# Four-tile layer blocks from one operand buffer in a recommender kernel: one comparison a step, one feature buffer, later reductions

## The chip, the cores and the metric

The kernel runs on one core of a Trainium2 chip. The metric is device time in microseconds (us), the median over several runs. Engines: PE (TensorE matmul), PEld (its weight loads), DVE (VectorE), ACT (ScalarE), POOL (GpSimd, which issues the gathers) and SP (SyncE, which issues the plain DMAs).

## What is computed

For each of 16384 rows: the mean of 32 rows of a 50000 x 300 table, the means of 20 rows of three tables of width 64, four single rows of width 64, all side by side (748 features), three relu layers and a sigmoid, with a "wide" sum of scalars added before the sigmoid.

```python
tok = word_emb[token_idx].mean(axis=1)
e1 = emb_mh1[mh1_idx].mean(axis=1)      # 1000 rows; mh2 5000, mh3 10000
...
o1 = emb_oh1[oh1_idx]                   # 100 rows; oh2 50, oh3 20, oh4 1000
...
emb = jnp.concatenate([tok, e1, e2, e3, o1, o2, o3, o4], axis=1)
wide = (wide_mh1[mh1_idx].sum(axis=(1, 2)) + ... + wide_oh4[oh4_idx][:, 0])[:, None]
h = jax.nn.relu(emb @ W1 + b1)          # 748 -> 1024
h = jax.nn.relu(h @ W2 + b2)            # 1024 -> 512
h = jax.nn.relu(h @ W3 + b3)            # 512 -> 256
return jax.nn.sigmoid(h @ Wd + bd + wide)
```

## The kernel before

A tile is 128 rows; there are 128 tiles. The kernel is one long schedule written out by hand (`manual_schedule`): a loop of 1424 steps, 11 to a tile and 16 more at the end (`WAKE`), in which the order of the calls is the order of the instructions on each engine. Every engine works off its own queue in order. Five streams run side by side, shifted against each other:

- **Token gather** (`tokens`, L249; `add_up`, L237). POOL issues 4096 indirect DMAs of 128 table rows (L259), two to a buffer `tok_rows`, with six buffers. Three groups of two later, DVE adds them up in `own` (L241, L243, L247); the last addition of a tile writes `g_tok`. The gathers are spread evenly over the steps.
- **Counts** (`one_hots`, L318; `counts`, L336). The small tables are not gathered. For each row, DVE compares its 64 keys with an iota (L326, twice a step: 6 rows of the low key, `row`, and 6 of the slice number, `slice`), ACT scales half of the `row` part (L333), PE multiplies the two (L344, 6 products a step), and ACT packs the counts into `cnt` (L347). `row` and `slice` have two buffers each; the comparison for step i+1 is issued in step i.
- **Sums from counts** (`small_sums`, L353). One tile later, PE multiplies the counts with the small tables kept on chip, 138 products a tile (L363), in four groups of fields, in the order of `SMALL`; each group collects in `pg`, which has one buffer, and DVE reduces it into the feature buffer `g` (L369). `sums_by_step` spreads them over the steps, one group's end to a step at most.
- **Transposes** (`Block.add_small`, L401; `Block.add_tokens`, L415). Four and three PE transposes per tile (L405, L408, L424, L425), evicted by DVE in three and two instructions (L409, L412, L413; L426, L427) into `x_small` and `x_tok`, which have two buffers each.
- **Layers** (`mlp`, L475; `layer`, L453). When the tiles of a block of three (`LAYER_TILES`) are in place, its 48 + 32 + 8 products and the two of the output run with 384 columns (L462, L487), ACT evicts each (L471), paced over the steps until the next block is due (`ready`, L547; `begin`, `left`). 42 blocks of three and two of one tile. If a block is not through when the next is ready, the rest is issued at once (`layers.finish`). The last tile's first three chunks are multiplied early (`early_part`, L435).

At the start, PE splits the small tables into three bf16 terms (`convert_tables`, L171), paced by `TABLE_PACE`. Index loads (`load_indices`, L270) are made once for four tiles on SP; `lookup_keys` and `key_columns` prepare their keys.

The functions, with the line numbers of the profile:

Of the kernel before, what the change touches and what calls it, by code (L numbers as in the profile page):

```python
# [8 lines left out]
F32 = mybir.dt.float32  # L9
# [16 lines left out]
TOK_BUFS = 6  # L26
WAKE = 16
EARLY = 3
BLOCK = 512
LAYER_TILES = 3  # L30
LAST_TILES = 2
# [8 lines left out]
TABLE_PACE = 1.3  # L40
# [5 lines left out]
SMALL = ("o4", "e1", "e2", "e3", "o1", "o2", "o3")  # L46
WIDE_IN_FRONT = ("mh1", "mh3", "oh2")
G_COLS = 7 * ROW
# [7 lines left out]
def kernel(  # L56
# [27 lines left out]
    tables = {"o4": oh4, "e1": mh1, "e2": mh2, "e3": mh3, "o1": oh1, "o2": oh2, "o3": oh3}  # L84
    slices, n_h = {}, 0
    for f in SMALL:
# [9 lines left out]
    ohp = ctx.enter_context(tc.tile_pool(name="onehot", bufs=2))  # L96
    cp = ctx.enter_context(tc.tile_pool(name="counts", bufs=2))
    gp = ctx.enter_context(tc.tile_pool(name="g", bufs=2))
    wp = ctx.enter_context(tc.tile_pool(name="wide", bufs=2))
    xsp = ctx.enter_context(tc.tile_pool(name="x_small", bufs=2))  # L100
    xtp = ctx.enter_context(tc.tile_pool(name="x_tok", bufs=2))
# [7 lines left out]

    chunk_rows = [  # L110
        [(300, 428)],
        [(428, 556)],
        [(556, 684)],
        [(684, 748), (256, 300)],
        [(0, 128)],
        [(128, 256)],
    ]
    chunk_k = [sum(b - a for a, b in rows) for rows in chunk_rows]
    NK = len(chunk_rows)

# [4 lines left out]
    scale = const.tile([P, 3], F32, name="scale")  # L125
# [3 lines left out]

# [18 lines left out]


# [61 lines left out]

# [9 lines left out]
    def load_weights():  # L221
        for k, rows in enumerate(chunk_rows):
            at = 0
            for a, b in rows:
                nc.sync.dma_start(out=w1_sb[at : at + b - a, k, :], in_=w1[a:b, :])
                at += b - a
        nc.sync.dma_start(out=w2_sb, in_=w2.rearrange("(k p) m -> p k m", p=P))
        nc.sync.dma_start(out=w3_sb, in_=w3.rearrange("(k p) m -> p k m", p=P))
        for sb, dram in ((wd_sb, wd), (b1_sb, b1), (b2_sb, b2), (b3_sb, b3), (bd_sb, bd)):
            nc.sync.dma_start(out=sb, in_=dram)  # L230

    n_groups = N_TOK // TOK_GROUP
    n_all = B // P * n_groups + TOK_LAG
    sums_of = {}
    token_indices = {}

    def add_up(t, q, rows):  # L237
# [4 lines left out]
        else:  # L242
            nc.vector.tensor_add(tok_sum, tok_sum, a)  # L243
            to = tok_sum
            if q == n_groups - 1:
                to = sums_of[t] = gp.tile([P, TOK_D], F32, name="g_tok")
# [23 lines left out]
    def load_indices(blk):  # L270
# [7 lines left out]
        ix = keyp.tile([P, NSUB // 2, 2, N_SMALL], I32, name="ix")  # L278
        for s in range(NSUB):
            nc.sync.dma_start(  # L280
                out=ix[(s % 2) * HALF : (s % 2 + 1) * HALF, s // 2],
# [7 lines left out]
    def lookup_keys(ix):  # L289

        pairs = NSUB // 2
        low = keyp.tile([P, pairs, 2, N_SMALL], I32, name="low", tag="low")
        nc.vector.tensor_single_scalar(low, ix, P - 1, op=ALU.bitwise_and)
        nc.vector.tensor_single_scalar(ix, ix, 7, op=ALU.logical_shift_right)
        keys = keyp.tile([P, pairs, 2, 2 * N_SMALL], BF16, name="keys", tag="keys")
        for r in range(pairs):
            view = keys[:, r].rearrange("p w (f c) -> p w f c", f=2)
            nc.vector.tensor_copy(view[:, 0], low[:, r])
            nc.vector.tensor_add(view[:, 1], ix[:, r], first)
        return keys  # L300

    def key_columns(keys):


        pairs = NSUB // 2
        pk = ps_h.tile([P, pairs, 2, P], BF16, name="pk", tag="ph")
        for r in range(pairs):
            for w in range(2):
                nc.tensor.transpose(pk[:, r, w, :], keys[:, r, w, :], ident_bf)
        sc = scp.tile([P, pairs, 2, 2, HALF, 2], BF16, name="sc")  # L310
        n = pairs * 2 * P
        nc.vector.tensor_copy(
            sc.rearrange("p r w t b d -> p (r w t b) d"),
            pk.rearrange("p r w b -> p (r w b)").unsqueeze(2).to_broadcast([P, n, 2]),
        )
        return sc

    def one_hots(sc, s, i):  # L318
# [3 lines left out]
        row1 = ohp.tile([P, ONEHOT, P], BF16, name="row1")  # L322
        slice1 = ohp.tile([P, ONEHOT, n_h], BF16, name="slice1")
        for w, (one, n) in enumerate(((row1, P), (slice1, n_h))):
            shape = [P, rows, n // 2, 2]
            nc.vector.tensor_tensor(  # L326
                one[:, 0:rows, :].rearrange("p i (n d) -> p i n d", d=2),
                iota[:, 0:n].rearrange("p (n d) -> p n d", d=2).unsqueeze(1).to_broadcast(shape),
                sc[:, s // 2, w, s % 2, b : b + rows, :].unsqueeze(2).to_broadcast(shape),
                ALU.is_equal,  # L330
            )
        upper = row1[HALF:P, 0:rows, :]
        nc.scalar.activation(upper, upper, AF.Copy, scale=UPPER)  # L333
        return row1, slice1

    def counts(cnt, hot, i):  # L336
# [5 lines left out]
        for k in range(rows):  # L342
            at = k % n * n_h
            nc.tensor.matmul(  # L344
                pc[:, k // n, at : at + n_h], hot[0][:, k, :], hot[1][:, k, :], start=True, stop=True
            )
# [6 lines left out]
    def small_sums(g, cnt):  # L353
# [3 lines left out]
        for i in (0, 2, 4, 6):  # L357
            pair = SMALL[i : i + 2]
            pg = ps_g.tile([P, 2, 3 * ROW], F32, name="pg")
            for j, f in enumerate(pair):  # L360
                h0, h1 = slices[f]
                for h in range(h0, h1):
# [3 lines left out]
                    yield 1  # L366
            at = i * ROW
            n = len(pair)
            nc.vector.tensor_reduce(  # L369
                g[:, at : at + n * ROW].rearrange("p (f d) -> p f d", f=n),  # L370
                pg[:, 0:n, :].rearrange("p f (c d) -> p f d c", c=3),
                AX.X,
                ALU.add,
            )
            yield None

    def wide_term(g):
# [4 lines left out]
            g[:, EMB : EMB + 6 * ROW].rearrange("p (c d) -> p c d", d=2 * ROW)[:, :, 0:2],  # L382
# [3 lines left out]
        nc.vector.tensor_add(g[:, EMB : EMB + 1], wide, g[:, G_COLS - 1 : G_COLS])  # L386

    class Block:
# [3 lines left out]
        def __init__(self, first, n):  # L392
            self.first, self.n, self.missing = first, n * P, 2 * n
            self.small = xsp.tile([P, 4, N], F32, name="x_small")
            self.wide = wp.tile([1, N], F32, name="wide_row")
            self.tok = None

        def columns(self, t):
            return slice((t - self.first) * P, (t - self.first + 1) * P)

        def add_small(self, t, g):  # L401

            at = self.columns(t)
            pt = ps_h.tile([P, 4, P], F32, name="pt", tag="ph")
            nc.tensor.transpose(pt[:, 3, :], g[:, 0:P], ident)  # L405
            for k in range(3):
                c = (1 + 2 * k) * ROW + 1
                nc.tensor.transpose(pt[:, k, :], g[:, c : c + P], ident)  # L408
            nc.vector.tensor_tensor(  # L409
                self.small[:, 0:3, at], pt[:, 0:3, :], scale.unsqueeze(2).to_broadcast([P, 3, P]), ALU.mult  # L410
            )
            nc.vector.tensor_copy(self.small[0:EMB, 3, at], pt[0:EMB, 3, :])  # L412
            nc.vector.tensor_copy(self.wide[:, at], pt[EMB : EMB + 1, 3, :])  # L413

        def add_tokens(self, t, g):  # L415


            if self.tok is None:
                self.tok = xtp.tile([P, 2, N], F32, name="x_tok")
            at = self.columns(t)  # L420
            rest = TOK_D - 2 * P
            pt = ps_h.tile([P, 3, P], F32, name="pt", tag="ph")
# [242 lines left out]
```

## Time and profile before

| what | value |
|---|---|
| median of 10 runs | 5194.51 us (5191.93 to 5196.4) |
| profiled execution | 5194.04 us, span from first to last instruction 5192.3 us |
| granted PE clock, mean | 0.983 |
| DMA | 652 MB, mean 126 GB/s |
| matmuls of the layers (L462) | 7744 records, two to each fp32 product |

The page lists busy times per engine, the span in 40 slices, the chain of work that ended last, and the costliest groups of instructions with the idle time in front of them and what ended it. Of the chain that ended last, PE has 28% of the span, DMA 25%, DVE 19%, "issue" 16% and POOL 9%. In a group's line the first number after the bar is the busy time in all, the second the mean length of one instruction in ns; overlapping matmuls make that length greater than the distance from one start to the next. Timeline lines read: start, length, engine, line, operation, number of instructions merged, and in brackets the idle time before and what ended it.

### The profile page before, as it was taken

What the parts mean: (1) busy time and instruction counts of PE and PEld (TensorE: products, weight loads), DVE (VectorE), ACT (ScalarE), POOL (GpSimd) and SP (SyncE); (2) the same over time, 40 slices, a digit from 0 to 9 for tenths busy, and PEclk for the clock granted to TensorE, in tenths of its full rate; (3) what the DMA queues carried; (4) which work ended last, traced back from release to release, by engine and by line L of the source; (5) the groups of instructions that cost most, each with busy time, mean ns of one, the idle gap of its engine ahead of it and who ended that gap; (6) DMA issues with size and microseconds to landing.
All of it is one profiled execution on the core that took longest, in us unless ns stands there. A gap on an engine that the chain in (4) does not pass through costs nothing.

```text
span 5192.3 us, 94821 instructions
## 1 busy us (share of the span) xinstructions
PE 4846.5 (93%) x34940; PEld 3557.5 (69%) x34940; DVE 3854.5 (74%) x8481; ACT 2758.4 (53%) x3538; POOL 3877.1 (75%) x4103
## 2 busy tenths in 40 slices
PE   7899999999999999999999999999999999999999
PEld 5676676667666766766776667666667666676667
DVE  7777777777777777777777777777777777777772
ACT  6555555555555555555555555555555555555551
POOL 7777777777777777777777777777777777777774
PEclk9999999999999999999999999999999999999999
DMA  7444444444444444444444444444444444444442
GB/s 198 124 126 126 124 127 126 124 125 126 125 124 125 126 125 125 127 126 124 126 125 126 124 125 126 126 124 127 125 124 126 125 125 124 125 126 126 124 124 67
DMA packets 252899, 652.00 MB, mean 126 GB/s; under 512 B 119035, under 2 KB 119591, under 8 KB 252435
## 3 DMA queue, kind: packets, MB, share of 16 engines
q0 software_dynamic: 196608, 629.41, 45.2%
q1 hardware_dynamic: 55827, 16.53, 1.4%
q8 instruction: 276, 4.52, 0.4%
q14 instruction: 188, 1.54, 0.1%
HBM read 645.59 MB, written 0.07 MB: 124 GB/s over the span
## 4 chain that ended last, share of the span: by engine, by line
PE 28%; DMA 25%; DVE 19%; issue 16%; POOL 9%; ACT 1%; DVEq 0%; SPq 0%; POOLq 0%; ACTq 0%
DMA tok_rows<-in_word_emb_dram,it 24%; PE ph L462 16%; POOL tok_rows L259 9%; PE pg L363 8%; DVE own L247 6%; DVE own L243 4%; DVE slice L326 3%; PE pc L344 2%; DVE row L326 2%; PE po L487 1%; DVE g L369 1%; DVE wide_row L413 0%; DVE own L241 0%; DVE x_small L427 0%; DVE x_small L412 0%
## 5 line engine op out<-in xcount | busy, mean ns | idle before, releaser
L259 POOL DMA_INDIRECT tok_rows<-in_word_emb_dram,it x4096 | 3876.2, 946 | 1277.9 <-issue 760.8
L333 ACT ACTIVATE row<-row 64x768 bf16<-64x768 bf16 (+1 forms) x1408 | 1155.3, 821 | 1570.6 <-DVE row L326 1551.9
L363 PE MATMUL pg<-terms,cnt 128*128 128x195 bf16 x17664 | 1764.1, 249 | 227.0 <-DVE g L369 225.9
L363 PEld LDWEIGHTS <-cnt 128*128 128x128 fp8e3 x17664 | 1529.0, 98 | 181.8 <-issue 175.1
L347 ACT ACTIVATE cnt<-pc 128x828 uint16<-128x828 f32 (+1 forms) x1408 | 1191.8, 846 | 165.3 <-PE pc L344 130.7
L462 PE MATMUL ph<-h,w_sb 128*128 128x384 f32 (+1 forms) x3520 | 1254.0, 495 | 0.5 <-ACT h L471 0.5
L247 DVE TENSOR_TENSOR own<-own,tok_rows 128x300 f32<-128x300 f32 x1792 | 856.9, 478 | 469.6 <-DMA tok_rows<-in_word_emb_dram,it 425.5
L243 DVE TENSOR_TENSOR own<-own,tok_rows 128x300 f32<-128x300 f32 x1920 | 918.0, 478 | 261.2 <-DMA tok_rows<-in_word_emb_dram,it 204.8
L462 PE MATMUL ph<-x_small,w_sb 128*128 128x384 f32 (+1 forms) x2784 | 1012.2, 488 | 6.2 <-DVE x_small L409 3.3
L344 PEld LDWEIGHTS <-row 128*128 128x128 bf16 x8192 | 599.9, 98 | 587.4 <-issue 282.5
L462 PEld LDWEIGHTS ph<-h,w_sb 128*128 128x128 f32 x3520 | 633.5, 197 | 387.0 <-issue 107.1
L326 DVE TENSOR_TENSOR row<-own,sc 128x768 bf16<-128x768 bf16 (+1 forms) x1408 | 761.8, 541 | 128.0 <-PE pc L344 28.5
L326 DVE TENSOR_TENSOR slice<-own,sc 128x828 bf16<-128x828 bf16 (+1 forms) x1408 | 795.9, 565 | 0.0
L344 PE MATMUL pc<-slice,row 128*128 128x138 bf16 x8192 | 740.7, 225 | 53.2 <-ACT row L333 52.5
L471 ACT ACTIVATE h<-ph,b_sb 128x384 f32<-128x384 f32 (+1 forms) x612 | 350.0, 572 | 626.0 <-PE ph L462 601.0
L462 PEld LDWEIGHTS ph<-x_small,w_sb 128*128 128x128 f32 x2784 | 487.3, 192 | 246.4 <-issue 21.1
L462 PE MATMUL ph<-x_tok,w_sb 128*128 128x384 f32 (+1 forms) x1392 | 533.7, 488 | 0.0
L369 DVE TENSOR_REDUCE g<-pg 128x130 f32<-128x390 f32 (+1 forms) x512 | 258.4, 505 | 95.8 <-PE pg L363 93.8
L462 PEld LDWEIGHTS ph<-x_tok,w_sb 128*128 128x128 f32 x1392 | 243.6, 192 | 113.5 <-issue 6.8
L241 DVE TENSOR_TENSOR own<-tok_rows 128x300 f32<-128x300 f32 x128 | 61.2, 478 | 116.9 <-DMA tok_rows<-in_word_emb_dram,it 115.9
L426 DVE TENSOR_SCALAR x_tok<-pt 128x256 f32<-128x256 f32 x128 | 53.6, 419 | 105.5 <-PE pt L425 105.4
L409 DVE TENSOR_TENSOR x_small<-pt,scale 128x384 f32<-128x384 f32 x128 | 70.2, 549 | 39.1 <-PE pt L408 37.6
(56 smaller groups left out, 875.4 us busy)
## 6 DMA issues: line engine op xcount, KB each, us to landing
tok_rows<-in_word_emb_dram,it POOLq DMA_INDIRECT x4096
ix<-in_idx_dram SPq DMA_DIRECT2D x128, 32.0 KB
w_sb<-in_W_dram SPq DMA_DIRECT2D x6, 512.0 KB
raw<-in_mh_dram SPq DMA_DIRECT2D x4, 682.5 KB
it<-in_idx_dram SPq DMA_DIRECT2D x32, 64.0 KB
w_sb<-in_W_dram SPq DMA_DIRECT2D x1, 2048.0 KB
out_dram<-h SPq DMA_DIRECT2D x42, 1.5 KB
raw<-in_mh_dram SPq DMA_DIRECT2D x2, 227.5 KB
```

The lines of the kernel that those rows point to most:

```text
L243: nc.vector.tensor_add(tok_sum, tok_sum, a)
L247: nc.vector.tensor_add(to, tok_sum, b)
L259: nc.gpsimd.indirect_dma_start(out=rows[:, r * TOK_D : (r + 1) * TOK_D], out_offset=None, in_=word, in_offset=bass.IndirectOffsetOnAxis(ap ...
L326: nc.vector.tensor_tensor(one[:, 0:rows, :].rearrange("p i (n d) -> p i n d", d=2), iota[:, 0:n].rearrange("p (n d) -> p n d", d=2).unsque ...
L333: nc.scalar.activation(upper, upper, AF.Copy, scale=UPPER)
L344: nc.tensor.matmul(pc[:, k // n, at : at + n_h], hot[0][:, k, :], hot[1][:, k, :], start=True, stop=True)
L347: nc.scalar.activation(cnt[:, :, b : b + rows].rearrange("l h (g k) -> l h g k", g=2), pc[:, :, 0 : n * n_h].rearrange("l g (k h) -> l h g ...
L363: nc.tensor.matmul(pg[:, j, :], by_slice[:, h, :], terms[:, h, :], start=(h == h0), stop=(h == h1 - 1))
L369: nc.vector.tensor_reduce(g[:, at : at + n * ROW].rearrange("p (f d) -> p f d", f=n), pg[:, 0:n, :].rearrange("p f (c d) -> p f d c", c=3) ...
L409: nc.vector.tensor_tensor(self.small[:, 0:3, at], pt[:, 0:3, :], scale.unsqueeze(2).to_broadcast([P, 3, P]), ALU.mult)
L462: nc.tensor.matmul(ph[:, 0:n], weights[: src.shape[0], k, m * P : (m + 1) * P], src, start=(k == 0), stop=(k == len(srcs) - 1),)
L471: nc.scalar.activation(dst[:, m, 0:n], ph[:, 0:n], AF.Relu, bias=bias[:, m : m + 1])
```

## The change

- **Layers.** Blocks of four tiles (512 columns), at the end blocks of 2, 1 and 1: 31 + 3 blocks. One operand `x` with one buffer in place of `x_small` and `x_tok`. A tile of the next block is transposed only when the current block's first layer has been issued (`free`); six transposes, one DVE eviction with a scale per chunk. The wide row goes through the operand as one row of chunk 3 (its weights are zero) and is copied out behind the first layer (`keep_wide`).
- **Features.** Sums and token sum share one buffer `g` (three of them).
- **One-hots.** One comparison a step for both parts, 2 x 6 x 138 elements, three buffers.
- **Sums.** The order of the fields and the steps at which their products are issued are given by tables (`early_sums`, before transposes and layers of the step; `late_sums`, behind them). The reduction of a group is not issued with its last product but at the end of the step or of the next (`later`, `flush`). The pair e1, o4 has 16 slices, e2, e3 119, o1, o2 two, o3 one; `large` is 20.
- **Layer evictions.** ACT's relu is issued in front of the last product of the next output, or behind the next one-hots (`pending`, `flush_outputs`).
- **Keys.** Indices are loaded and keys prepared for two tiles at a time. `TABLE_PACE` is 1.5.

The diff, cut to its core:

```diff
+HOT_BUFS = 3
-BLOCK = 512
-LAYER_TILES = 3
-LAST_TILES = 2
+BLOCK = 256
+LAYER_TILES = 4
+LAST_BLOCKS = (2, 1, 1)
-TABLE_PACE = 1.3
+TABLE_PACE = 1.5
-SMALL = ("o4", "e1", "e2", "e3", "o1", "o2", "o3")
+SMALL = ("e1", "o4", "e2", "e3", "o1", "o2", "o3")
...
-    gp = ctx.enter_context(tc.tile_pool(name="g", bufs=2))
-    wp = ctx.enter_context(tc.tile_pool(name="wide", bufs=2))
-    xsp = ctx.enter_context(tc.tile_pool(name="x_small", bufs=2))
-    xtp = ctx.enter_context(tc.tile_pool(name="x_tok", bufs=2))
+    gp = ctx.enter_context(tc.tile_pool(name="g", bufs=3))
+    wp = ctx.enter_context(tc.tile_pool(name="wide", bufs=1))
+    xp = ctx.enter_context(tc.tile_pool(name="x", bufs=1))
...
     def load_weights():
+        nc.vector.memset(w1_sb[0:1, 3, :], 0.0)
...
-        row1 = ohp.tile([P, ONEHOT, P], BF16, name="row1")
-        slice1 = ohp.tile([P, ONEHOT, n_h], BF16, name="slice1")
-        for w, (one, n) in enumerate(((row1, P), (slice1, n_h))):
-            shape = [P, rows, n // 2, 2]
-            nc.vector.tensor_tensor(
...
+        hot = ohp.tile([P, 2 * ONEHOT, n_h], BF16, name="hot")
+        shape = [P, 2 * rows, n_h // 2, 2]
+        at = s * HALF + b
+        nc.vector.tensor_tensor(
+            hot[:, 0 : 2 * rows, :].rearrange("p i (n d) -> p i n d", d=2),
...
     def small_sums(t, cnt):
...
+            def evict(pair=pair, n=n, pg=pg):
+                nc.vector.tensor_reduce(
+                    field_columns(features(t), pair),
+                    pg[:, 0:n, :].rearrange("p f (c d) -> p f d c", c=3),
...
-                    yield 1
...
-            yield None
+                    yield evict if f == pair[-1] and h == h1 - 1 else None
...
     class Block:
         def __init__(self, first, n):
-            self.small = xsp.tile([P, 4, N], F32, name="x_small")
+            self.x = xp.tile([P, NK, N], F32, name="x")
+            self.read = False
+        def transpose(self, t, ks):
...
+            if banks > 1:
+                two = ps_c.tile([P, 2, 512], F32, name="pc")
+            else:
+                two = ps_h.tile([P, 1, n * P], F32, name="pt", tag="ph")
...
+            for j, k in enumerate(ks):
+                c = chunk_at[k]
+                nc.tensor.transpose(pt[:, j // n, j % n, :], g[:, c : c + P], ident)
+            def evict():
+                nc.vector.tensor_tensor(
+                    self.x[:, ks[0] : ks[-1] + 1, at : at + P].rearrange("p (a c) b -> p a c b", a=banks),
...
+        def keep_wide(self):
+            self.wide = wp.tile([1, N], F32, name="wide_row")
+            nc.vector.tensor_copy(self.wide[:, 0 : self.n], self.x[0:1, 3, 0 : self.n])
+            self.read = True
...
     def layer(dst, weights, bias, srcs, n_out, part=None):
+                if k == len(srcs) - 1:
+                    flush_outputs()
...
-            nc.scalar.activation(dst[:, m, 0:n], ph[:, 0:n], AF.Relu, bias=bias[:, m : m + 1])
+            def evict(m=m, ph=ph):
+                nc.scalar.activation(dst[:, m, 0:n], ph[:, 0:n], AF.Relu, bias=bias[:, m : m + 1])
+            pending.append(evict)
...
+    n_of = {f: slices[f][1] - slices[f][0] for f in SMALL}
+    sizes_of_pairs = [sum(n_of[f] for f in SMALL[i : i + 2]) for i in (0, 2, 4, 6)]
+    large = -(-sizes_of_pairs[1] // 6)
+    early_sums = {1: sizes_of_pairs[0], 9: sizes_of_pairs[2], **{i: large for i in range(3, 8)}}
+    late_sums = {2: large, 10: sizes_of_pairs[3]}
...
+    def run_sums(gen, n, step, due):
+        for _ in range(n):
+            evict = next(gen, None)
+            if evict:
+                later.append((due, evict))
+    def flush(step):
+        for entry in [e for e in later if e[0] <= step]:
+            later.remove(entry)
+            entry[1]()
...
+        if sums:
+            run_sums(sums, early_sums.get(i, 0), step, step)
         if waiting and step >= waiting[0][0]:
-            block = transpose(*waiting.pop(0)[1:])
-            if block:
+            _, k, ks = waiting[0]
+            free = k in block_of or not current or current.read
+            if free and (k in summed or ks[0] < N_EARLY and k == tiles - 1):
+                waiting.pop(0)
+                block = block_for(k)
+                later.append((step, block.transpose(k, ks)))
+                if not block.missing:
+                    flush(step)
...
         toks.to(n_all * (step + 1) / n_steps)
...
         if layers:
             layers.to(mlp_work * layers.size * (step + 1 - begin) / left + ahead)
+        if sums:
+            run_sums(sums, late_sums.get(i, 0), step, step + 1)
+        flush(step)
```

## The prediction

> **What bounds the kernel now.** I read the page first, then the timeline of POOL, the waits, the engines' busy time by stretches, and the timelines of PE and DVE over the last 130 us. The page alone points to PE:
>
> ```profile
> PE 4846.5 (93%) x34940; PEld 3557.5 (69%) x34940; DVE 3854.5 (74%) x8481; ACT 2758.4 (53%) x3538; POOL 3877.1 (75%) x4103
> L259 POOL DMA_INDIRECT tok_rows<-in_word_emb_dram,it x4096 | 3876.2, 946 | 1277.9 <-issue 760.8
> ```
>
> But POOL's 1277.9 us of idle time are no slack. Its timeline, in the middle and near the end (start, duration, idle before):
>
> ```profile
> 2003.06 0.95 POOL L259 DMA_INDIRECT tok_rows<-in_word_emb_dram,it  x1 [0.30 <-DMA tok_rows<-in_word_emb_dram,it]
> 2004.31 0.95 POOL L259 DMA_INDIRECT tok_rows<-in_word_emb_dram,it  x1 [0.30 <-DVE own L247]
> 2005.56 0.94 POOL L259 DMA_INDIRECT tok_rows<-in_word_emb_dram,it  x1 [0.30 <-issue]
> ...
> 5135.86 0.94 POOL L259 DMA_INDIRECT tok_rows<-in_word_emb_dram,it  x1 [16.76 <-DVE own L247]
> ```
>
> Every gather is followed by 0.30 us, whatever is named as releaser, so gathers start every 1.251 us, and 4096 of them take 5124 us from the first start at 3.15. Beyond that POOL loses 4.4 us in two stalls before 85 us, about 4 us to scattered long gathers, and 24.5 us in stalls after 5087. **POOL is the clock of the kernel until about 5060 us; PE decides after that.** The stretches (length, then busy time of PE, PEld, DVE, ACT, POOL, then the granted PE clock):
>
> ```profile
> 4200.00:5000.00 800.00, 748.35 (x5428) 549.41 (x5427) 603.09 (x1329) 428.00 (x545) 605.19 (x640) 0.99 0.47 125
> 5060.00:5164.00 104.00, 101.94 (x609) 74.56 (x607) 38.82 (x89) 21.73 (x40) 53.89 (x57) 1.00 0.32 87
> 5164.00:5192.30 28.30, 22.94 (x158) 21.49 (x156) 1.00 (x3) 5.54 (x15) 0.00 (x0) 0.82 0.00 1
> ```
>
> PE has 6% to spare in the run and 2% from 5060 to 5164. There DVE idles behind PE, and POOL behind DVE (the 16.76 above). The last 28 us are one tile's chain. So what the change saves in the run is worth nothing, and what it does to PE's work after about 4975 us is worth its full price.
>
> **PE's prices**, from the timeline (a fp32 product is two records):
>
> ```profile
> 5106.49 1.46 PE L363 MATMUL pg<-terms,cnt 128*128 128x195 bf16 x15
> 5107.79 5.35 PE L462 MATMUL ph<-h,w_sb 128*128 128x384 f32 x16
> 5112.97 1.46 PE L363 MATMUL pg<-terms,cnt 128*128 128x195 bf16 x15
> ...
> 5148.88 6.86 PE L462 MATMUL ph<-h,w_sb 128*128 128x128 f32 x60
> 5155.58 0.27 PE L405 MATMUL pt<-ident,g 128*128 128x128 f32 x1
> ```
>
> Start to start: a slice sum 1.30/15 = 0.087 us; a 384-column product 2 x 5.18/16 = 0.648; a 128-column one 2 x 6.70/60 = 0.223; counts 0.063 and transposes 0.110 each in the same way. 512 columns are not in the trace: between 0.648 (nothing added) and 1.295 (twice 384). The line through 128 and 384 gives 0.860, and 0.436 for 256; I take these.
>
> **The parts that the run hides.** Per 128 columns the layers cost 90 x 0.860/4 = 19.4 us of PE against 19.4 before: no gain. Six transposes a tile for seven save 0.11 us of PE a tile. One comparison of 1656 elements for two: the rows of 768, 828, 512 and 552 elements (0.554, 0.578, 0.413, 0.433 us) grow by 0.525 ns an element, so 1.01 us, bounded by 0.578 and by the 1.13 of both old ones; one eviction of 128x768 for five (0.55+0.27+0.29+0.42+0.29) between 0.55 and 1.10, by halves 0.95. DVE, 74% busy, waits for gathers in its free time, so these save nothing while POOL sets the pace; without that cover each would be worth under 1 us a step or tile. ACT's evictions grow from 0.58 to about 0.69 us and become fewer (47% idle). The index loads on SP become twice as many and half as large, 22 steps ahead of use; the memset of one weight row comes once. The faster table pace moves PE work earlier at the start: steps 12 to 16 end some 3 to 5 us later by PE's rows, a third one-hot buffer gives a step (3.6 us) back, and the key columns wait behind it; I keep the 4.4 us of early stalls, with 0 and 8 as ends.
>
> POOL is held back only when an addition comes late: a gather's rows are added 2.95 us after its issue at best (median over additions that waited for it), and six buffers allow 13.8 us less the addition. So DVE may be 10.3 us late. At a block switch in the changed order DVE evicts the last transposes, then waits for the old block's last two products of layer 3 and the two output products (4 x 0.86): about 6 us late. Covered; if the cover fails, see the rivals.
>
> **Later reads.** Today PE waits for the reductions of `pg`:
>
> ```profile
> PE pg L363 <- DVE g L369: 225.9, 177, 3.6
> ```
>
> This is slack being spent, not time lost. The change wants it gone, but in the built order it is not: 6 x 20 slices are asked for where the pair e2, e3 has 119, so the 120th is o1's, in the same step, directly behind e3's last; and two are asked for in step 9, o2 and o3. Both o1 and o3 need the single `pg` buffer that DVE must first reduce. What a turn costs when nothing else is late, early in the run:
>
> ```profile
> 83.92 1.37 PE L363 MATMUL pg<-terms,cnt 128*128 128x195 bf16 x14
> 85.32 0.56 DVE L369 TENSOR_REDUCE g<-pg 128x130 f32<-128x390 f32 x1 [3.52 <-PE pg L363]
> 85.94 0.33 PE L363 MATMUL pg<-terms,cnt 128*128 128x195 bf16 x2 [0.29 <-DVE g L369]
> ```
>
> The fourteen products are through PE at 83.92 + 14 x 0.087 = 85.14, and the next pair's first starts at 85.94 (count products ran in between): a turn of 0.80 us. Two a tile: free in the run (lower end 0), paid where PE is the bound.
>
> **One operand instead of two.** A block's operand is refilled only behind the previous first layer (48 of 90 products, about half a block's steps), so three tiles wait, their features in three buffers; the fourth tile's transposes, eviction and start follow at the switch, under 4 x 0.86 us of the old block. PE's loss: 0 by that cover, at most 0.66 + 0.95 us a block without it; I take 0. *The Trainium skill* ("Trainium Kernel Development and Optimization", Best Practices) asks for double buffers and so speaks against this; the row nearest to it is PE's 3.3 us in all behind the small operand's eviction today, with two buffers, no row shows a single one, and if the rule held at every one of 34 switches it would be 34 x 1.6 = 55 us of PE time, most of it in the run's slack.
>
> **The end, where it is decided.** Blocks of four start when the fourth tile's token sum is there. Tile 123's sum ends at 4974.3:
>
> ```profile
> 4973.80 0.47 DVE L247 TENSOR_TENSOR g_tok<-own,tok_rows 128x300 f32<-128x300 f32 x1 [1.50 <-DMA tok_rows<-in_word_emb_dram,it]
> ```
>
> Gathers do not move, so the changed kernel's block 120 to 123 starts after that: six transposes 0.7 and four products 3.4 give 4978.5 (step 1379). The next block, of 2 tiles, starts at step 1402: 77 us of layers in 23 steps instead of the usual 44. PE is asked for 77.4/23 + 1.5 (counts, sums, transposes) = 4.9 us a step; POOL's pace is 3.60 (2051 groups of two gathers in 1424 steps). From 4978.5 to the last tile's second transposes the built PE queue holds 90 products of 512, 90 of 256 and 102 of 128 columns (77.4 + 39.2 + 22.8 = 139.4 us), 162 count products (10.2), 476 slice sums (41.4), 21 + 2 transposes (2.4): **193.4 us**. The same tally for the old kernel from 5062.3 gives 98.5 where the trace has 100.1 (to 5162.4), waits included: times 1.016, 196.5. Eight turns of `pg` (tiles 124 to 127) are new: 6.4. PE is through at 4978.5 + 196.5 + 6.4 = 5181.4, the old one at 5162.4. In the old order 172 us were left at 4979, since a third of a later block was already done.
>
> DVE is behind PE there and POOL behind DVE, as now; the last gathers then land a few us before PE is through. In the changed DVE queue four additions (4 x 0.51) stand between the previous block's output addition and the last sum, and PE meanwhile has twelve early products (2.7 us): PE waits 0 to 1 us, I take 0.
>
> **The tail.** Now:
>
> ```profile
> 5163.61 0.44 PE L424 MATMUL pt<-ident,g_tok 128*128 128x128 f32 x2 [1.26 <-DVE g_tok L247]
> 5165.00:5170.00 5.00, 4.08 (x18) 3.50 (x18) 0.00 (x0) 1.10 (x3) 0.00 (x0) 0.55 0.00 0
> ```
>
> 28.7 us from there to the end, of which the clock record has 5165.5 to 5175.8 at half speed, after 3.4 us in which PE was busy for 39%. Half of 10.3 us is 5.1 lost. In the changed order the 1.26 us wait is gone and only the eviction (0.8 us) interrupts PE, about 75% busy; in the trace windows that preceded a half clock were at most 51% busy. So 28.7 - 5.1 = 23.6, upper end 28.7. *The Trainium skill* ("TensorE: Matmul & The Clock Gate", Part 1) says that the clock halves after an idle window of about 3.4 us; the row shows a half clock without any such gap, so the measurement decides; by the rule the changed tail would be at full clock too, and the sum the same.
>
> Sum: 5181.4 + 23.6 = 5205.0 of span. The profiled run took 5194.04 at a span of 5192.3, so 1.7 more: **5207 us**, 13 above its own 5194.04; the median of the runs, 5194.51, lies 0.5 beside it.
>
> **Rivals.** (a) *Same*: DVE, idle then, turns `pg` around unseen, and waits do not scale: 5207 - 6.4 - 3.1 = 5197, or 5193 with the early stalls gone too. For it: o3's turn has only a short product before it. Against: one buffer, strict order. Chance 0.22. (b) *Faster*: PE's backlog does not form, because PE enters step 1379 ahead or the blocks at the end overlap more than the queue shows. Then POOL runs through: last gather at 5130, last sum at 5133, tail 23.6 to 28.7: 5158 to 5163 with the 1.7. It decides if PE's work after 4978 is under 155 us instead of 193; against it stands the tally, good to 2% on the old end. Chance 0.10. (c) *Much slower*: at block switches DVE is over 10.3 us late, 31 times 1 us or more: 5238 and up. For it: additions already come up to 8.5 us after their earliest time in the run. Against: the 6 us above. Chance 0.10. (d) Within the forecast: half clock in the tail, 5212.
>
> **Numbers.** Forecast 0.58, around 5207: from 5198 (turns cheaper) to 5220 (half clock, 8 us of early stalls, last sum late). With (a) and a part of (c) the range is 5192 to 5224. A measurement of this kernel tells no more than about 0.2%, 10.4 us: same is 5184 to 5205. Slower: 0.43 of the forecast, 0.10 of (c), 0.02 of (a): 0.55. Faster: (b) and a little: 0.11. Same: 0.34.
>
> **What will show it.** Gathers still 1.251 us apart with no stall from 200 to 5060; PE's wait for the reduction of `pg` larger, not smaller, with some 3 us once a tile; PE without a gap over 1 us from about 4979; POOL stalls of 20 us and more after 5060; the last transposes near 5182. The forecast is wrong if POOL ends by 5135, if PE has gaps after 4990, or if the gathers' pitch changes.

## The result, and the profile after

The changed kernel takes 5217.72 us (median of 8 runs, 5216.83 to 5218.45); the kernel before took 5194.48 in 28 runs beside it. The ratio is 1.0045, with a 95% interval of 1.0036 to 1.0054: slower by 0.45%, more than the 0.2% that a measurement can tell from no change. The profiled execution took 5218.31 us at a span of 5216.5, 24.2 us more than before. Beside the experiments below the kernel before took 5191.84 to 5196.94 us (medians), and on one chip far more, so ratios to the kernel before, run beside, are compared.

The page after, PE and the gathers:

```profile
PE 4812.7 (92%) x33012; PEld 3200.9 (61%) x33012; DVE 3744.8 (72%) x6686; ACT 2688.3 (52%) x3388; POOL 3881.0 (74%) x4103
L279 POOL DMA_INDIRECT tok_rows<-in_word_emb_dram,it x4096 | 3880.1, 947 | 1305.1 <-issue 786.3
```

Every engine but POOL is busy for less time than before: PE by 34 us, DVE by 110, ACT by 70. The kernel is slower all the same. POOL's timeline tells where (start, duration, idle before):

```profile
64.28 0.94 POOL L279 DMA_INDIRECT tok_rows<-in_word_emb_dram,it  x1 [6.55 <-DVE own L260]
84.02 0.94 POOL L279 DMA_INDIRECT tok_rows<-in_word_emb_dram,it  x1 [5.03 <-DVE own L267]
...
2003.69 0.95 POOL L279 DMA_INDIRECT tok_rows<-in_word_emb_dram,it  x1 [0.30 <-issue]
2004.95 0.95 POOL L279 DMA_INDIRECT tok_rows<-in_word_emb_dram,it  x1 [0.30 <-issue]
...
5062.72 0.94 POOL L279 DMA_INDIRECT tok_rows<-in_word_emb_dram,it  x1 [10.35 <-DVE own L267]
5086.30 0.94 POOL L279 DMA_INDIRECT tok_rows<-in_word_emb_dram,it  x1 [5.86 <-DVE own L267]
5109.19 0.94 POOL L279 DMA_INDIRECT tok_rows<-in_word_emb_dram,it  x1 [10.69 <-DVE own L267]
```

In the run the gathers still start every 1.251 us. The stalls lie before 85 us and behind 5000; the first of the later ones ends at 5032.7 (3.37 us of idle time). The span can be added up exactly from POOL's rows: the start of the first gather, 4095 times 1.251 (5122.8), what gathers lost beyond this pitch, and the time from the start of the last one to the end. "Early" is the loss of the first 120 gathers, "run" of gathers 120 to 3600, "end" of the rest. The column "overload" will be explained with the experiments. Each row is one profiled execution, and the executions ran on several chips.

| kernel | blocks at the end | first | early | run | end | after the last gather | span | overload |
|---|---|---|---|---|---|---|---|---|
| before | ..3, 1, 1 | 3.2 | 4.8 | -0.4 | 24.2 | 37.7 | 5192.3 | 35.5 |
| after | ..4, 2, 1, 1 | 2.8 | 11.1 | 3.6 | 45.3 | 30.9 | 5216.5 | 48.3 |
| ends_3311 | ..4, 3, 3, 1, 1 | 3.0 | 10.9 | -0.4 | 37.8 | 30.7 | 5204.9 | 45.0 |
| ends_gradual | ..4, 3, 3, 2, 2, 2, 1, .. | 2.9 | 10.3 | 0.8 | 34.5 | 28.0 | 5199.4 | 38.4 |
| blocks_of_3 | ..3, 1, 1 | 2.9 | 9.9 | 0.1 | 29.9 | 30.6 | 5196.3 | 35.5 |
| blocks_of_2 | ..2, 1, 1 | 2.8 | 10.9 | 0.9 | 11.8 | 30.4 | 5179.6 | 16.1 |
| before_blocks_of_2 | ..2, 1, 1 | 3.0 | 4.8 | 3.4 | 8.5 | 35.9 | 5178.6 | 16.1 |
| combined_2 | ..2, 1, 1 | 2.9 | 7.2 | 2.5 | 7.7 | 28.9 | 5172.0 | 16.1 |
| pg_turns | ..4, 2, 1, 1 | 3.0 | 10.2 | -1.2 | 38.5 | 29.3 | 5202.7 | 48.3 |
| table_pace | ..4, 2, 1, 1 | 2.9 | 6.8 | 1.7 | 46.5 | 30.9 | 5211.6 | 48.3 |
| blocks_of_1_pg | all 1 | 2.9 | 11.0 | 19.8 | 0.3 | 32.2 | 5189.0 | 0 |

So of the 24.2 us between before and after, +21.1 come from stalls at the end, +6.3 from the start, +4.0 from the run and -6.8 from the way behind the last gather (-0.3 from the first gather; rounding makes up the rest).

PE's waits for the reduction of `pg` (total us, times, longest) grew, as forecast:

```profile
PE pg L397 <- DVE g L387: 300.7, 258, 3.4
PE ph L496 <- DVE x L440: 36.2, 22, 3.5
```

The timeline of PE at the start of the block of tiles 120 to 123 shows both turns of one tile:

```profile
5003.14 1.80 PE L397 MATMUL pg<-terms,cnt 128*128 128x195 bf16 x19
5005.59 0.24 PE L397 MATMUL pg<-terms,cnt 128*128 128x195 bf16 x1 [0.65 <-DVE g L387]
...
5008.64 4.51 PE L496 MATMUL ph<-x,w_sb 128*128 128x512 f32 x10
5012.99 0.52 PE L362 MATMUL pc<-hot 128*128 128x138 bf16 x6
5013.35 0.24 PE L397 MATMUL pg<-terms,cnt 128*128 128x195 bf16 x1
5014.25 0.24 PE L397 MATMUL pg<-terms,cnt 128*128 128x195 bf16 x1 [0.66 <-DVE g L387]
```

PE issues the nineteen last slices of the second pair, then sits idle for 0.65 us before o1's single product, because DVE must empty the one `pg` buffer first; 9 us later the same before o3. From 4986 to 5185 these eight waits (two a tile, four tiles) are the only gaps of PE above 0.5 us.

### The profile page after: what moved, and what is told of

It reads as the page before. It is cut to its first block, busy times and chain, and to the rows that moved or that the text cites. A ratio compares the mean times of both kernels' runs of the same rounds, so it can differ in the third digit from the quotient of the medians.

```text
span 5216.5 us, 88327 instructions
## 1 busy us (share of the span) xinstructions
PE 4812.7 (92%) x33012; PEld 3200.9 (61%) x33012; DVE 3744.8 (72%) x6686; ACT 2688.3 (52%) x3388; POOL 3881.0 (74%) x4103
## 4 chain that ended last, share of the span: by engine, by line
PE 52%; DMA 16%; DVE 14%; issue 10%; POOL 6%; ACT 1%; DVEq 0%; POOLq 0%; ACTq 0%
PE ph L496 29%; DMA tok_rows<-in_word_emb_dram,it 16%; PE pg L397 16%; POOL tok_rows L279 6%; DVE hot L344 5%; PE pc L362 5%; DVE own L267 3%; DVE own L262 2%; DVE g L387 2%; PE po L528 1%; PE pc L436 1%; DVE x L440 1%; ACT cnt L365 0%; ACT hot L351 0%; PE left L211 0%
## 5 line engine op out<-in xcount | busy, mean ns | idle before, releaser
L351 ACT ACTIVATE hot<-hot 64x768 bf16<-64x768 bf16 (+1 forms) x1408 | 1155.3, 821 | 1723.5 <-DVE hot L344 1707.6
L496 PE MATMUL ph<-x,w_sb 128*128 128x512 f32 (+4 forms) x3216 | 1486.8, 589 | 36.6 <-DVE x L440 36.2
L344 DVE TENSOR_TENSOR hot<-own,sc 128x1656 bf16<-128x1656 bf16 (+1 forms) x1408 | 1393.1, 990 | 88.6 <-PE pc L362 7.2
L496 PE MATMUL ph<-h,w_sb 128*128 128x512 f32 (+2 forms) x2720 | 1243.2, 584 | 0.5 <-ACT h L507 0.5
L362 PEld LDWEIGHTS <-hot 128*128 128x128 bf16 x8192 | 602.9, 98 | 784.5 <-issue 641.6
L496 PEld LDWEIGHTS ph<-x,w_sb 128*128 128x128 f32 (+1 forms) x3216 | 550.1, 193 | 589.4 <-issue 537.6
L362 PE MATMUL pc<-hot 128*128 128x138 bf16 x8192 | 735.9, 225 | 43.9 <-ACT hot L351 36.8
L496 PEld LDWEIGHTS ph<-h,w_sb 128*128 128x128 f32 x2720 | 464.0, 193 | 465.7 <-issue 462.2
L507 ACT ACTIVATE h<-ph,b_sb 128x512 f32<-128x512 f32 (+2 forms) x472 | 313.8, 665 | 199.7 <-PE ph L496 191.5
L440 DVE TENSOR_TENSOR x<-pc,scale 128x768 f32<-128x768 f32 x127 | 120.9, 952 | 96.6 <-PE pc L436 96.5
```

Of the source, the lines that this page charges most:

```text
L344: nc.vector.tensor_tensor(hot[:, 0 : 2 * rows, :].rearrange("p i (n d) -> p i n d", d=2), iota.rearrange("p (n d) -> p n d", d=2).unsqueez ...
L362: nc.tensor.matmul(pc[:, k // n, at : at + n_h], hot[:, 2 * k, 0:P], hot[:, 2 * k + 1, :], start=True, stop=True)
L496: nc.tensor.matmul(ph[:, 0:n], weights[: src.shape[0], k, m * P : (m + 1) * P], src, start=(k == 0), stop=(k == len(srcs) - 1),)
L507: nc.scalar.activation(dst[:, m, 0:n], ph[:, 0:n], AF.Relu, bias=bias[:, m : m + 1])
```

## The experiments

**Whose end is it? Last blocks as before.** The changed kernel, one line:

```diff
-LAST_BLOCKS = (2, 1, 1)
+LAST_BLOCKS = (3, 3, 1, 1)
```

> The changed kernel with its last blocks cut as in the kernel before: ..., 3, 3, 1, 1 tiles instead of ..., 4, 2, 1, 1. Theory A (the loss lies in the PE work left behind the last blocks): the last three-tile block starts when tile 125's token sum is there, some 10.5 us later than the 5062 of the kernel before (6 of them early stalls, 4 longer gathers); its 100 us of PE work and four turns of pg of 0.65 us put the last transposes near 5174, the tail of 24 us the time near 5200, 18 us under the changed kernel. Rival B (the loss is spread over the 34 block switches, each with its single operand to refill): the last blocks move little, 5213 to 5218.

Measured: 5206.62 us, ratio 1.0030 (1.0018 to 1.0041). The kernel before took 5191.84 on this chip, so the changed kernel would be near 5215: the edit gains 9 us, half of what theory A asked for. Rival B is out, as block switches are the same until 4900. But POOL has a new stall, ending at 4961 us, where the block of four is followed by one of three. It stands first here; the second line is the longest stall of the fall from three tiles to one:

```profile
4961.44 0.94 POOL L279 DMA_INDIRECT tok_rows<-in_word_emb_dram,it  x1 [7.92 <-DVE own L260]
...
5152.89 0.94 POOL L279 DMA_INDIRECT tok_rows<-in_word_emb_dram,it  x1 [18.19 <-DVE own L267]
```

**A gentler slope.**

```diff
-LAST_BLOCKS = (2, 1, 1)
+LAST_BLOCKS = (3, 3, 2, 2, 2, 1, 1, 1, 1)
```

> The changed kernel with last blocks of 3, 3, 2, 2, 2, 1, 1, 1, 1 tiles behind those of four. Theory A: per tile the layers take 19.5 us of the 39.6 us that the gathers of one tile take, counts and sums 17; a block that is one tile larger than its successor leaves 9 to 16 us of PE work behind, an equal successor takes 3.3 us a tile off, so some 6 us are left behind the last sum, which comes near 5146 (5124 of gathers, 11 early stalls, 4 long gathers, 2.8 at the start, 3 to the last addition): 5146 + 6 + 24 + 1.7 = 5178, with 5170 to 5190 as ends. Rival B (loss spread over block switches): there are six more of them, 5217 or more.

Measured: 5201.16 us, ratio 1.0017 (1.0008 to 1.0026). It is the right direction, but 23 us above the expected time. POOL's timeline shows why: it stalls at each place where the size falls, 4 to 3, 3 to 2 and 2 to 1. These are the longest rows of the three places:

```profile
4642.35 0.94 POOL L279 DMA_INDIRECT tok_rows<-in_word_emb_dram,it  x1 [6.59 <-DVE own L260]
...
4854.43 0.94 POOL L279 DMA_INDIRECT tok_rows<-in_word_emb_dram,it  x1 [9.40 <-DVE own L260]
...
5067.65 0.94 POOL L279 DMA_INDIRECT tok_rows<-in_word_emb_dram,it  x1 [12.22 <-DVE own L260]
```

What failed was the idea that an equal successor works a backlog off. PE's slack does return then, but POOL has stalled meanwhile, and POOL, with no slack of its own, cannot catch up. Hence theory A2: *each fall from n to m tiles costs its own overload*. The layers of n tiles (n x 19.4 us) must be done in the time of m tiles, of which counts, sums and transposes leave PE 39.6 - 16.9 = 22.7 us each. (39.6 us are 11 steps of 3.60; the 32 gathers of a tile take 32 x 1.251 = 40.0, which would make an overload smaller by some 0.2 to 0.4 us for each of the m tiles.) The overload is 19.4 n - 22.7 m: 9.5 us for 4 to 3, 12.8 for 3 to 2, 16.1 for 2 to 1, 35.5 for 3 to 1, 32.2 for 4 to 2. The table holds the sums: the measured stalls at the end lie 2 to 11 us below them, in the same order. ends_gradual shows the falls one by one: around its three places POOL loses 9.8, 12.0 and 13.0 us, where A2 has 9.5, 12.8 and 16.1. So it is the falls to a single tile that cost less than their overload. The rows of the changed kernel with o1 and o3 behind one `pg` also hold some 5 us of its turns, which A2 leaves out: without them, in pg_turns, the end is 38.5, 9.8 below the sum. What hides the rest (by the prediction DVE may be some 10 us late before POOL stalls) was not tried by itself.

**Blocks of three, of two, of one.** These tell A2 from losses in the run. In the changed kernel `LAYER_TILES` and `LAST_BLOCKS` were set to 3 and (1, 1), 2 and (1, 1), 1 and (1,); the last one also has the edit of the next experiment. In the kernel before:

```diff
-LAYER_TILES = 3
+LAYER_TILES = 2
```

> The changed kernel with blocks of three tiles and 1, 1 at the end, as in the kernel before; all else of the change stays. Theory A2 (each time a block is followed by a smaller one, PE is asked for the larger one's layers in the smaller one's time, n x 19.4 - m x 22.7 us too much, POOL stalls by about that and cannot get it back): one shrinking 3 to 1 of 35 us as in the kernel before, so its time of 5192 on this chip, plus 6.5 us more early stalls, plus six turns of pg of 0.65, less 4.7 for the tail at full clock: 5197 or so. Rival B2 (the single operand, the one comparison, or the later reads lose time in the run): 5203 or more.

> The changed kernel with blocks of two tiles and 1, 1 at the end. Theory A2: only one shrinking, 2 to 1, 16 us of overload, of which DVE's lateness of up to 10 us hides a part. The last two-tile block starts near 5063 (gather 4032 at 1.251 us each, 11 us of early stalls), the kernel before needed 100 us from there with one tile's layers (19.4) more: last transposes near 5063 + 80.7 + 4 = 5148, tail 24, plus 1.7: 5174, with 5168 to 5182 as ends. Rival G (twice the block switches, each a wait for the refilled operand, make DVE late and POOL stall in the run): 5200 or more, with stalls of POOL between 200 and 5000.

> The kernel before with blocks of two tiles instead of three, nothing else. Theory A2: the shrinking 2 to 1 leaves 16 us instead of 35: from the start of the last two-tile block at 5062 PE needs 100.1 - 19.4 = 80.7 us, last transposes near 5144, tail 24 to 28.7: 5169 to 5174, less 2.6 on this chip. Rival: the 16.45 and 7.75 us stalls of POOL near the end come from the last tiles' own additions, not from PE's backlog: 5188 to 5192.

> The changed kernel with a block for every tile, and the late request of the second pair cut to 19 slices. Theory A2: nothing shrinks, no overload; POOL runs through after its early stalls, last gather near 5140, last sum 5143, last transposes 5145, tail 24: 5171, as long as PE's work a tile, 90 x 0.223 + 11 x 0.38 + 138 x 0.087 + 0.7 + one refill of 1.6 = 38.5 us, stays under the 39.6 of the gathers. Rival G (switches cost more than 2.7 us a tile): PE sets the pace, every 0.1 us a tile above 39.6 is 13 us, POOL stalls all through the run, 5200 and more.

The kernel before took 5196.77 us on this chip. Measured: blocks_of_3 took 5203.24, ratio 1.0012 (1.0003 to 1.0021); its profiled execution, at 5198.04, is its fastest, so its row in the table flatters it by 5 us. The expectations were written from a chip with 5192 for the kernel before: A2's 5197 is 5 us above that, B2's 5203 is 11. Measured are 6.5 above the kernel before beside it. The interval, 2 to 11 us, has room for A2's 5 and hardly for B2's 11, and the row shows a loss of 0.1 us in the run: A2 holds, and nothing else of the change costs much.

blocks_of_2 took 5184.63, ratio 0.9975 (0.9964 to 0.9985), and before_blocks_of_2 took 5179.69, ratio 0.9963 (0.9950 to 0.9977): both beat the kernel before. A2's direction is right in both, its times are some 10 us too low. Half of this is that the kernel before takes 5 us more here than the 5192 that I started from. In the profiled execution of blocks_of_2 the last two-tile block starts 4 us later than I put it, and from there to the last transposes PE takes 89 us instead of 84.7; why was not followed up. The stalls that are left, of blocks_of_2 first, then of before_blocks_of_2:

```profile
5127.94 0.94 POOL L279 DMA_INDIRECT tok_rows<-in_word_emb_dram,it  x1 [10.28 <-DVE own L267]
```

```profile
5123.92 0.95 POOL L259 DMA_INDIRECT tok_rows<-in_word_emb_dram,it  x1 [7.73 <-DVE own L247]
```

blocks_of_1_pg took 5193.46, ratio 0.9993 (0.9984 to 1.0002), where A2 had 5171 and rival G 5200 or more. It has no stall at the end, as A2 has it, but loses 19.8 us in the run, nearly all in 34 small stalls, as rival G has it. Each is right in part. With a block for each tile PE waits 92 times for the refilled operand (137 us, 1.5 each), and has this little to spare (stretch 1200 to 3200: length, busy PE, PEld, DVE, ACT, POOL, clock):

```profile
1200.00:3200.00 2000.00, 1899.34 (x19521) 1841.11 (x19519) 1467.66 (x2672) 1179.24 (x1859) 1504.89 (x1591) 1.00 0.46 125
```

95% against 93% in the changed kernel and in the blocks of three and two. With 34 switches the price of a single operand, 1.5 us a switch, hides in PE's slack; here, I think, it can no longer hide whole. The kernel before speaks for this: with two operands its PE is busy for 94.5% of the same stretch, and it loses nothing in the run. But one-tile blocks also have products of fewer columns and more evictions, and the operand was not tried by itself.

**The turns of `pg`.** The late request asks only for what the pair has left:

```diff
-    late_sums = {2: large, 10: sizes_of_pairs[3]}
+    late_sums = {2: sizes_of_pairs[1] - 5 * large, 10: sizes_of_pairs[3]}
```

> The changed kernel with the late request of the second pair cut to the 19 slices that the pair has left, so that o1 comes in step 9 with o2 and o3 alone in step 10, each behind a reduction that is a step old. Theory A: the eight gaps of 0.65 us behind the last blocks go, 5.2 us: 5212.5; the sum of PE's waits for the reduction falls from 301 us to under 100, and the 290 us of them before 4980 are worth nothing. Rival C (DVE turns pg around unseen, other waits take their place): 5217 to 5218. Rival D (the turns also cost in the run): 5200 or less.

Measured: 5204.11 us, ratio 1.0024 (1.0014 to 1.0033), 11 us under the changed kernel instead of 5.2, between theory A and rival D.

```profile
PE pg L397 <- DVE g L387: 51.5, 66, 2.1
```

The eight gaps are gone: from the transposes of tile 123 to the last ones PE takes 200.6 us instead of 206.3, so 5.7. Another 2.5 us come from the start of that stretch: PE reaches these transposes 3.3 us behind the last gather of tile 123 instead of 5.8; why was not followed up. In the profiled executions, which lie 13.8 us apart, the rest is early stalls (0.9) and the run (4.8), where gathers were shorter (see the last section). Rival C is out. So is rival D: in the run the changed kernel has no stall over 0.4 us beyond the pitch that the edit could have taken away. Of 249 us of waits taken away in the run and at the end, some 8 count.

**The early stalls.** First the pace alone (table_pace, the first two lines below), then with the key columns later as well (all runs from early_stalls on, but for two_compares):

```diff
-TABLE_PACE = 1.5
+TABLE_PACE = 1.32
...
-        if t < tiles and more and s == 1 and i == 5:
+        if t < tiles and more and s == 1 and i == 9:
```

> The changed kernel with the pace of the tables at 1.32 instead of 1.5 pieces a step. Theory A: by step 16 PE has 2.5 pieces of 2.2 us less behind it, DVE's waits for the first reduction and the first key columns end 5.5 us earlier, and the stalls of POOL before 85 us fall from 11.0 to about 5.5 us; all of it reaches the end: 5212. Rival E (the stalls come from the order of the reductions and key columns, whatever the pace): stalls stay at 9 us and above, 5216 to 5218.

Measured: 5211.79 us, ratio 1.0039 (1.0025 to 1.0053); by this alone it can't be told from the changed kernel. The early loss did fall, from 11.1 to 6.8 us, 1.3 more than theory A had it:

```profile
66.71 0.94 POOL L279 DMA_INDIRECT tok_rows<-in_word_emb_dram,it  x1 [1.42 <-DVE own L267]
77.69 0.95 POOL L279 DMA_INDIRECT tok_rows<-in_word_emb_dram,it  x1 [3.77 <-DVE own L267]
87.36 0.94 POOL L279 DMA_INDIRECT tok_rows<-in_word_emb_dram,it  x1 [2.47 <-DVE own L267]
```

DVE waits behind PE's table work for the first reduction (10.0 us), for a step of the tables themselves (3.4), for the key columns (5.2) and for the second reduction (4.0).

> The changed kernel with the pace of the tables at 1.32 and the key columns of the next two tiles taken in the ninth step of the odd tile instead of the fifth (both only ever late at the start). Theory A: with the pace alone POOL's early stalls were 6.8 us, 3.5 of them DVE's wait for the key columns behind PE's table work; these go: stalls of about 3.5 us, the ratio to the kernel before falls from 1.0045 to 1.0031 (7.5 us). Rival E2 (the wait moves on to the next reduction): stalls stay near 6.8, ratio 1.0039.

> The changed kernel with its one comparison of a step made as two of half the elements. Theory A (what DVE saves in the run is worth nothing): DVE's busy time grows by about 0.14 us x 1408 = 190 us, additions come a little later, no new stall of POOL: the ratio to the kernel before stays at 1.0045, 1.0035 to 1.0055. Rival F (DVE's load already makes gathers late): 20 us or more slower, stalls of POOL between 200 and 4950.

> The changed kernel with blocks of 2 and 1, 1 at the end, the late request cut to 19 slices, the pace of 1.32 and the key columns in the ninth step. If the terms add up: ratio 0.9975 of the blocks of two, less 0.0014 of the early stalls, less 0.0010 to 0.0016 of the turns of pg: 0.995, 5168 to 5172. The floor is POOL's: 2.9 + 5124 + 3.5 + 3 for the last gather, 3 to the last sum, 24 of tail, 1.7: 5162. If the turns' slack was taken up by the smaller blocks already: 0.996, 5177.

These three ran on a chip on which the kernel before took 7218 us, and they answer none of their questions: ratios 1.0221, 1.0481 and 1.0667. There PE's granted clock was 0.84 to 0.87, that of the kernel before included, and the waits (here of early_stalls) hold rows that the other runs lack:

```profile
ACT cnt L365 <- remote: 1683.7, 251, 15.2
PE pg L397 <- issue: 798.0, 1038, 4.3
```

All four engines stood still together for over 0.5 us some 250 to 280 times in each run (290 to 320 us; once in the profiled runs of after and combined_2), and POOL of early_stalls waited 2040 us for additions. Whether the second comparison costs anything where nothing disturbs is therefore open. The sum of the edits was run once more:

> The kernel of the run combined once more, on a chip where the kernel before takes its 5190 to 5197 us. If the terms add up: early stalls of POOL of 3.5 instead of 11 us; no gap of 0.65 us behind the last blocks; 5124 + 2.9 + 3.5 + 3 put the last gather at 5134 to 5140 (some of the 2-to-1 stall of 10 us left), the last transposes near 5145, the tail of 24 the time at 5168 to 5172, ratio 0.995. Rival E2 (the early wait moves on to the next reduction, stalls near 6.8) and slack already taken up: 5177, ratio 0.996 to 0.9965.

Measured: 5173.74 us, ratio 0.9957 (0.9943 to 0.9970), 23 us under the kernel before and the lowest ratio of all. The terms add up nearly, to 0.7 per mille short of 0.995. But the interval overlaps with that of before_blocks_of_2 (0.9950 to 0.9977): one number changed in the kernel before gains about as much as the whole change with its four repairs, and these runs can't tell the two apart. Its stalls:

```profile
67.58 0.94 POOL L279 DMA_INDIRECT tok_rows<-in_word_emb_dram,it  x1 [1.70 <-DVE own L267]
87.61 0.94 POOL L279 DMA_INDIRECT tok_rows<-in_word_emb_dram,it  x1 [5.31 <-DVE own L267]
5121.83 0.94 POOL L279 DMA_INDIRECT tok_rows<-in_word_emb_dram,it  x1 [7.45 <-DVE own L267]
```

The early loss is 7.2 us: with the key columns out of the way DVE waits for the second reduction instead (9.1 us, until 84.8). Rival E2 was right: what is late is PE's table work, and moving one reader of it moves the wait.

## Why the prediction was right, step by step

The forecast was 5207, 13 us above before; measured are 5217.7, 23 above. The mechanism was right, the start of PE's last stretch was mis-sized by 12 us, half of it by the early stalls, and the reasons behind two more terms were too narrow or wrong.

**POOL sets the pace in the run: right.** The pitch is unchanged and between 85 and 5000 no gather loses more than 0.4 us beyond it. All that PE, DVE and ACT saved is worth nothing there.

**The early stalls: mis-sized.** I kept 4.4 us with 0 and 8 as ends; by the same measure 4.8 became 11.1, outside these ends. I had worked out that PE's steps 12 to 16 end 3 to 5 us later, and then let a third one-hot buffer give a step back. The third buffer did not help, as DVE's next instruction in order was the reduction: DVE waited 10.3 us for it and began it at 58.45, where the kernel before began its first one at 50.52 after a wait of 3.45.

```profile
58.45 0.56 DVE L387 TENSOR_REDUCE g<-pg 128x130 f32<-128x390 f32 x1 [10.31 <-PE pg L397]
```

With the pace at 1.32 the loss was 6.8, so 4.3 of the 6.3 extra belong to the pace. As POOL has no slack, the whole sum reaches the end: tile 123's token sum ends at 4984.9 instead of 4974.3.

```profile
4984.39 0.47 DVE L267 TENSOR_TENSOR g<-own,tok_rows 128x300 f32<-128x300 f32 x1 [1.63 <-DMA tok_rows<-in_word_emb_dram,it]
```

Of these 10.6 us, 6 are early stalls and 4 longer gathers in the run, an increase I hadn't counted at all. That it came with this execution and not with the change is likely (last section), but not shown.

**PE's work behind 4978: right to half a per cent.** Forecast from the block's first product to the last transposes: 196.5 + 6.4 = 202.9 us. Measured: from 4990.6 to the start of the last transposes at 5192.6, 202.0. A product of 512 columns, interpolated at 0.860 us, takes 0.870 (two records; ten take 4.35 from 5008.64 to 5012.99). The turns of `pg`, put at 0.80, took 0.655: 5.2 us instead of 6.4. The start was 12.1 us late: the 10.6 above, and 1.5 for slice sums that PE still had in front of the block's last transposes:

```profile
4984.58 1.89 PE L397 MATMUL pg<-terms,cnt 128*128 128x195 bf16 x20
4986.30 0.82 PE L436 MATMUL pc<-ident,g 128*128 128x128 f32 x6
```

**The tail: right.** 23.6 us forecast from the start of the last transposes, 23.9 measured, all at full clock:

```profile
5192.60:5216.50 23.90, 18.99 (x161) 17.66 (x159) 1.05 (x3) 5.55 (x15) 0.00 (x0) 1.00 0.00 1
```

PE is busy for 79% of it, where I had 75. In blocks_of_1_pg PE waited 4.6 us for the last token sum ahead of the same tail, the clock then stood at 0.5 for some 13 us, and the tail took 28.7. *The Trainium skill* ("TensorE: Matmul & The Clock Gate", Part 1) has the clock halved after an idle window of about 3.4 us; this run agrees with it, while the half clock in the tail of the kernel before came behind a wait of no more than 1.26 us.

**One operand at no cost: right in sum, wrong in reason.** I let four products of the old block cover the refill. They did not in 22 cases: PE waited 36.2 us, 1.6 each, which is what I had as the price without cover. It cost nothing that can be seen, as the row of blocks_of_3 has no loss in the run; PE's slack took it. *The Trainium skill* ("Trainium Kernel Development and Optimization", Best Practices) asks for double buffers, there to overlap DMA with compute; the runs say what the lack of one between engines costs: nothing that can be seen at 34 switches and PE at 93%, and at 128 switches and 95% at most the 20 us lost in the run.

**The last blocks: right, but explained too narrowly.** I counted what PE still had to do at the end and called it a backlog. The runs with other ends show that it is not the amount left, but each fall in block size: where a smaller block follows, POOL stalls, and a stall is final even if PE catches up. So POOL's stalls began at 5032.7, before the 5060 that I had named.

**Rivals.** (a) is out: `pg`'s turns were there and cost 5.7 us in PE's last stretch. (b) is out: PE's work in the last stretch was 202 us and not under 155. (c) is out: no stall in the run. (d) is out: no half clock in the tail.

**Small readings.** The second early stall of the kernel before ends at 87.9 us, not before 85, and its stalls at the end are 24.2 us, not 24.5. Neither changes the sum.

## What to carry to other kernels

When one engine paces a kernel without slack, add up its own rows (pitch, stalls, the way behind its last instruction): they give the span to the microsecond, and here 34 us of PE's busy time and 110 of DVE's saved elsewhere did not appear in them. Work that is batched over n tiles and must finish while m < n tiles pass overloads its engine once at each such fall. Small blocks throughout can beat large blocks with a short end, as blocks of two did here; with blocks of one, losses in the run took most of the gain back. A wait may be worth nothing 250 times in the run and its full price 8 times behind the point where another engine takes over, so count waits by stretch and not by total.

## What was not expected of the hardware

The mean duration of a gather differed a little between the profiled executions. Over gathers 120 to 3900, without those over 1 us, it was 0.9454 us in the kernel before, 0.9462 in the changed one, 0.9455 in blocks_of_2 and 0.9467 in before_blocks_of_2. One and the same kernel shows both ends on two chips: 0.9453 in combined (on the disturbed chip below) and 0.9464 in combined_2. Over 3780 gathers the range is up to 5 us, as much as several of the effects looked for; between before and after it is 3 of the 4.0 us lost in the run. With one trace a kernel, what sets it stays open.

On the disturbed chip the order of the kernels turned around: the version with the lowest ratio elsewhere was the slowest of the four, 6.7% behind the kernel before. What stopped the engines there stays open.
